# Second attention: the PSUM results of the side products are read one step later

## The chip, the cores and the metric

The kernel runs on one core of one Trainium2 chip. It is judged by its device time in microseconds (us), and the smaller is the better. Three runs of the kernel before gave 7818.84, 7816.00 and 7815.46 us; the median is 7816.0 us. One further execution was recorded by the hardware profiler: its time is 7809.57 us, and its span from the first instruction to the last is 7807.8 us.

## The reference

The program is a chain of four parts over 16 sequences of 512 tokens with 128 features. The change lies in the third part, which shares its stretch of time with the fourth.

```python
x = x + _L0_attn_ref(xn, ...) + _L0_ffn_ref(xn, ...)      # parts 1 and 2: four layers of scan + attention, ternary FFN
xn = _layernorm(x, axis=-1)
x = x + _L1_attn_ref(xn, ...) + _L1_ffn_ref(xn, Wr, W1, W2)

# part 3, _L1_attn_ref: 16 heads of 64, windows of 128 tokens
q, kv = x @ Wq, x @ Wkv                       # keys are also the values
q, kv = rotary(q) * SCALE, rotary(kv)
lkv = layernorm(look_around(kv))              # this window and the one before it
lsim = einsum('bwid,bwjd->bwij', q, lkv)      # masked: later tokens, before the start
pkv = softmax(kv by segments of 16 @ Wproj)   # one summary key for each segment
gkv = layernorm(sum of kv in a segment * pkv)
gsim = einsum('bnd,brd->bnr', q, gkv)         # masked: segments not finished
attn = softmax(concat([gsim, lsim]))
out = einsum(attn, concat([gkv, lkv])) @ Wout + bout

# part 4, _L1_ffn_ref: each token goes to one of 8 experts (argmax of softmax(x @ Wr)), at most 1024 for each
h = maximum(xe @ W1, 0);  ye = h @ W2         # xe: the tokens of one expert
y[token] = ye * p_token
```

## The kernel before

Parts 1 and 2 fill the first 5620 us and are not touched. Parts 3 and 4 are one block of code with an order written out by hand: the engines' queues hold the instructions in the order in which the Python code issues them, and each engine takes its queue in order.

Part 3 is cut into 64 **units** of 128 tokens (`u`; four of them, `t` = 0 to 3, make one sequence of 512), and a unit into four **groups** of four heads. The main loop runs over the groups `i`. In one turn it issues, with a call of `work(1)` after each piece:

- `scores(i)`: four matmuls `s` into PSUM tiles of pool `a_s` (five banks). VectorE reads each of them with the mask and takes the maximum (L1360, tiles `pr` and `am`), ScalarE makes the exponentials (L1361) and a copy `pg` of the summary columns (L1365). In a unit with `t` = 0 the rows are shorter.
- `weights_by_key(i - 1, two)`, twice: TensorE transposes (`gp` L1376 once, `pp` L1383), VectorE copies `gt` (L1378), ScalarE copies `pt` (L1385). `gp` and `pp` come from the same five banks as `s`; as seven tiles are taken in a turn, the first `pp` of a turn takes the bank of that turn's first `s`, and so waits until VectorE has read it.
- `values(i - 2, two)`, twice: the matmuls `o`, of which the first reads the summary values `gvb`; ScalarE copies `ot` (L1414) after every second group.

With a last `work(1)` this makes six steps in a turn and 24 in a unit.

Everything else is a **side product**, and is written as a generator in a list `streams`. `work(n)` goes through the list, resumes each generator that is due, and stops at the first one that answers with a positive number: that one has used the step. `yield 2` means "I have used this step; resume me two steps on", `yield -2` the same without using the step, `yield 0` "again at once". The generators, in the order of the list:

- `back(u)`: row sums to every lane by way of memory (`rd` L1424, L1426), then on GpSimd `ot` times their reciprocals (L1440), then the output projection: nine matmuls `po`, and VectorE's sum `ro` (L1447).
- `front(u)`: from the load of `xu` to the keys. Two products `kv` (read by VectorE, L1192 `by_cos`, and ScalarE, L1193 `raw`), four `q` (VectorE, L1210), GpSimd's rotary arithmetic (L1196 `raw`, L1199 and L1200 `kv`, L1218 `qt`), VectorE's `hm` (L1221) and `hd` (L1223), ScalarE's `hq` (L1229), GpSimd's `by_w` (L1227), VectorE's `hv` (L1232) and `pl` (L1244), the transposes `plt` (L1250, which reads `pl`; VectorE then makes `n` L1253, `smx` L1255 and `se` L1257) and `nt` (L1271, which read `n`; ScalarE L1272), `pwp` (L1283; VectorE `sw` L1285), the summary product `gp` into an `m` tile (VectorE L1298 to L1301), its norm on GpSimd (L1307 to L1314, tile `gv`), its transpose `gkt` (L1320; ScalarE L1327), and the DMAs `gv` (L1318) and `gvb` (four, L1333).
- `other_weights`, then `routing()`: it scatters the tokens to their experts (L1089, L1091) and then runs the 16 expert halves, each with one product `xep` (ScalarE L1122), four `hp` (ScalarE L1128) and one `yp` (VectorE L1135).
- `results()`, last: when the experts are done it gathers each token's expert row with a GpSimd DMA (`gy` L1147), loads `res` (L1154), adds them on VectorE (L1156) and stores `out` (L1157).

All side products share a pool of two banks, `a_m` (tiles `m_...`), in turn: a product can't begin until the product two before it has been read.

In the queues of the kernel before, the instructions that read a side product stand directly behind its matmuls, in the same resumption:

Of the kernel before, what the change touches and what calls it, by code (L numbers as in the profile page):

```python
# [69 lines left out]
def tile_kernel(  # L70
# [55 lines left out]
    with (  # L126
# [648 lines left out]
        tick = [0]  # L775
# [169 lines left out]
    with (  # L945
# [57 lines left out]
        def mm(out, lhsT, rhs, first=True, last=True):  # L1003
            nc.tensor.matmul(out, lhsT=lhsT, rhs=rhs, start=first, stop=last)  # L1004

        experts_done = [False]
        stored = [0]

        def routing():
# [8 lines left out]
            def big(i):  # L1018
                return space[:, i]
# [32 lines left out]
            total = misc("total")  # L1052
            mm(total, ones, hot2)
            tot = big(3)
            nc.vector.tensor_copy(tot, total.rearrange("p (t e) -> p t e", e=E))
            yield 1
            cum = pr.rearrange("p t e -> p (t e)").rearrange("p (e t) -> p e t", e=E)
# [7 lines left out]
            before = misc("before")  # L1065
            mm(before, const("tri"), hot2)
            rank = big(2)
            nc.vector.tensor_tensor(rank, cum.rearrange("p e t -> p t e"), tot, ALU.subtract)
            nc.vector.tensor_tensor(rank, rank, before.rearrange("p (t e) -> p t e", e=E), ALU.add)
            yield 1  # L1070
            nc.vector.tensor_tensor(rank, rank, hot, ALU.mult)
# [33 lines left out]
        def expert_half(e, hf):  # L1105
            nm = f"{e}_{hf}"
            if hf == 0:
                w1_sb = wk.tile([P, F1], F32, name=f"w1_{e}", tag="racc", bufs=1)
                nc.sync.dma_start(w1_sb, w1[e])
                w2_sb = wk.tile([P, 4, D], F32, name=f"w2_{e}", tag="x4", bufs=1)  # L1110
                nc.sync.dma_start(w2_sb, w2[e].rearrange("(c p) d -> p c d", p=P))
                expert_half.w = (w1_sb, w2_sb)
            w1_sb, w2_sb = expert_half.w
            at = e * CAP + hf * S
            xe = wk.tile([P, TB, D], F32, name=f"xe_{nm}", tag="x3", bufs=1)
            nc.sync.dma_start(xe, xe_d[at : at + S, :].rearrange("(t p) d -> p t d", p=P))
            yield -3
            ps = misc(f"xep_{nm}")
            for t in range(TB):
                nc.tensor.transpose(ps[:, t * P : (t + 1) * P], xe[:, t, :], ident)  # L1120
            xeT = wk.tile([P, S], F32, name=f"xeT_{nm}", tag="xt", bufs=1)
            nc.scalar.copy(xeT, ps)  # L1122
            yield 2
            he = wk.tile([P, 4, S], F32, name=f"he_{nm}", tag="he", bufs=1)
            for f in range(4):
                hp = misc(f"hp_{nm}_{f}")
                mm(hp, w1_sb[:, f * P : (f + 1) * P], xeT)
                nc.scalar.activation(he[:, f, :], hp, AF.Relu)  # L1128
                yield 1 + f // 3
            yp = misc(f"yp_{nm}")  # L1130
            for t in range(TB):
                for f in range(4):
                    mm(yp[:, t * P : (t + 1) * P], he[:, f, t * P : (t + 1) * P], w2_sb[:, f, :], f == 0, f == 3)
            ye = wk.tile([P, TB, D], F32, name=f"ye_{nm}", tag="d3", bufs=1)
            nc.vector.tensor_copy(ye, yp.rearrange("p (t d) -> p t d", d=D))  # L1135
            yield 2
            nc.sync.dma_start(ye_d[at : at + S, :].rearrange("(t p) d -> p t d", p=P), ye)
# [29 lines left out]
        def front(u):  # L1167
# [20 lines left out]
            for c in range(2):  # L1188
                ps = misc(f"kv_{u}_{c}")
                mm(ps, x, wkv_sb[:, c * S : (c + 1) * S])  # L1190
                psh = ps.rearrange("p (h d) -> p h d", d=DH1)
                nc.vector.tensor_tensor(halves(by_cos[:, 8 * c : 8 * c + 8]), halves(psh), table("cosk"), ALU.mult)  # L1192
                nc.scalar.copy(raw[:, 8 * c : 8 * c + 8], psh)  # L1193
                yield 1
            sink = const("sink")[:, t * 32 : (t + 1) * 32].unsqueeze(1).unsqueeze(1).broadcast_to(pair)
# [6 lines left out]
            for c in range(2):  # L1202
                parts = []
                for a, name in enumerate(("cosq", "sinq")):
                    ps = misc(f"q_{u}_{c}_{a}")
                    for i in range(4):
                        at = (4 * c + i) * P
                        mm(ps[:, i * P : (i + 1) * P], wq_sb[:, a, at : at + P], x)
                    q = wk.tile([P, 4, P], F32, name=f"q_{u}_{c}_{a}", tag=f"q{a}", bufs=2)
# [7 lines left out]
                    yield 1  # L1217
                nc.gpsimd.tensor_tensor(U.qt[:, 4 * c : 4 * c + 4, :], parts[0], parts[1], ALU.add)  # L1218
# [30 lines left out]
            ps = misc(f"plt_{u}")  # L1249
            nc.tensor.transpose(ps[0:H1, 0:P], pl, ident)  # L1250
            plv = ps[0:H1, 0:P].rearrange("p (s i) -> p s i", i=SEG)
            n = wk.tile(heads, F32, name=f"n_{u}", tag="hq", bufs=1)
# [6 lines left out]
            U.normed = True  # L1259
            yield 2  # L1260
            ss = wk.tile([H1, n_seg], F32, name=f"ss_{u}", tag="ss")
# [4 lines left out]
            for c in range(2):  # L1266
                ps = misc(f"nt_{u}_{c}")
                n2 = n.rearrange("p h d -> p (h d)")
                for i in range(4):
                    at = (4 * c + i) * P  # L1270
                    nc.tensor.transpose(ps[:, i * P : (i + 1) * P], n2[:, at : at + P], ident)  # L1271
                nc.scalar.activation(  # L1272
                    lkts[b % 2][:, 4 * c : 4 * c + 4, t * KW : t * KW + P],
                    ps.rearrange("p (i t) -> p i t", t=P),
                    AF.Identity,
                    scale=g_col,
                    bias=b_col,
                )
                yield 1
# [3 lines left out]
            nc.tensor.transpose(ps[:, 0:H1], se.rearrange("p s i -> p (s i)"), ident[0:H1, 0:H1])  # L1283
            sw = wk.tile([P, 4, 4, 32], F32, name=f"sw_{u}", tag="sw", bufs=1)
            nc.vector.tensor_tensor(  # L1285
# [4 lines left out]
            )  # L1290
            yield 2

            gp = misc(f"gp_{u}")
            for j in range(4):
                for g in range(4):
                    mm(gp[32 * g : 32 * g + 32, 0:DH1], sw[:, g, j, :], kv[:, 4 * g + j, :], j == 0, j == 3)
            gm = wk.tile([P, 1], F32, name=f"gm_{u}", tag="gm")
            nc.vector.tensor_reduce(gm, gp[:, 0:DH1], AX.X, ALU.add)  # L1298
# [4 lines left out]
            nc.scalar.activation(gq, gd, AF.Square, scale=DH1**-0.5)  # L1303
            yield 1
            gr = wk.tile([P, 1], F32, name=f"gr_{u}", tag="gr")
# [13 lines left out]
            ps = misc(f"gkt_{u}")  # L1319
            nc.tensor.transpose(ps[:, 0:P], gv.rearrange("p a d -> p (a d)"), ident)  # L1320
            for a in range(2):
                r = slice(64 * a, 64 * a + 64)
# [4 lines left out]
                nc.scalar.copy(to, keys.unsqueeze(2).broadcast_to([64, NHP, n, n_seg]))  # L1327
            yield 1
            yield -2
# [87 lines left out]
        def back(u):  # L1417
# [5 lines left out]
            ps = misc(f"rd_{u}")  # L1423
            nc.tensor.transpose(ps[0:H1, 0:P], U.sum, ident)  # L1424
            rd = wk.tile([H1, P], F32, name=f"rd_{u}", tag="rd", bufs=2)
            nc.vector.tensor_copy(rd, ps[0:H1, 0:P])  # L1426
            yield 2
            nc.sync.dma_start(rd_d[u % 2], rd)
# [14 lines left out]
            for i in range(NHP):  # L1443
                mm(po[:, 0:D], U.ot[:, i, :], wout_sb[:, i, :], i == 0, False)
            mm(po[:, 0:D], x1, ident, False, True)
            res = wk.tile([P, D], F32, name=f"ro_{u}", tag="ro", bufs=2)
            nc.vector.tensor_tensor(res, po[:, 0:D], bout_row, ALU.add)  # L1447
            yield 2
            nc.sync.dma_start(r_d[u * P : (u + 1) * P, :], res)
# [161 lines left out]
```

## Time and profile before

| What | Value |
|---|---|
| Median of three runs | 7816.0 us |
| Profiled execution: its time, its span | 7809.57 us, 7807.8 us |
| Parts 3 and 4: from about 5620 us to the end | some 2188 us |
| TensorE, VectorE, ScalarE, GpSimd busy, 7200 to 7400 us | 181.25, 133.06, 128.13, 142.45 us of 200 |
| The same, 6400 to 6600 us (experts running) | 189.36, 112.64, 123.06, 109.97 us of 200 |
| Granted TensorE clock, 6400 to 6600, 6800 to 7000, 7200 to 7400 us | 0.99, 0.86, 0.95 |

A line of the list of waits names who waited, for whom, the sum in us, how often and the longest. A line of the timeline gives the start, the length, the engine, the line, the operation and its tiles; the bracket is the engine's idle time before it and what ended it. A line of a table of stretches gives busy time and the number of instructions for each engine, and then the granted clock, where 1.00 is full speed.

### The profile page before, as it was taken

How to read it: one execution, taken by the hardware profiler on the slowest of the kernel's cores; microseconds unless marked ns; L12 is line 12 of the kernel's file. 1: busy time of each engine (PE TensorE's matmuls, PEld its weight loads, DVE VectorE, ACT ScalarE, POOL GpSimd, SP SyncE). 2: the span in 40 equal slices, each digit the busy share in tenths (PEclk: the TensorE clock that was granted, in tenths of full speed). 3: DMA queues.
4: the chain of work that ended last, by engine and by line, in shares of the span. 5: the costliest groups of instructions: out<-in, count | busy, mean ns of one | idle time of the engine just before them, and what ended most of it. 6: DMA issues, size and time to landing. Idle time of an engine off the chain costs nothing. (4 is left out here: it accounts for less than half of the span.)

```text
span 7807.8 us, 107882 instructions
## 1 busy us (share of the span) xinstructions
PE 7008.5 (90%) x38168; PEld 3232.4 (41%) x38168; DVE 4784.4 (61%) x9622; ACT 4616.8 (59%) x9357; POOL 3012.7 (39%) x3763
## 2 busy tenths in 40 slices
PE   6898999999999999999999999999678999888988
PEld 2233333333333333333333333333356666656666
DVE  4565666566666666566666666666366555666665
ACT  3565655666555666666666566656355666556666
POOL 3333332232223233222221222222268655667775
PEclk7899999999999999999999999999789999989999
DMA  2222222212222221122212222222211111111111
GB/s 70 78 83 65 75 70 66 84 64 69 68 71 69 70 66 64 65 64 71 69 61 65 66 74 80 77 77 91 78 33 50 49 42 49 40 46 32 34 35 36
DMA packets 394204, 491.18 MB, mean 63 GB/s; under 512 B 82240, under 2 KB 277952, under 8 KB 392512
## 3 DMA queue, kind: packets, MB, share of 16 engines
q1 hardware_dynamic: 389568, 475.89, 19.5%
q0 software_dynamic: 4096, 8.40, 0.4%
q8 instruction: 302, 4.95, 0.3%
q14 instruction: 238, 1.95, 0.1%
HBM read 348.35 MB, written 132.64 MB: 62 GB/s over the span
## 5 line engine op out<-in xcount | busy, mean ns | idle before, releaser
L921 DVE TENSOR_REDUCE nm<-n 128x1 f32<-128x512 f32 x4096 | 2588.3, 683 | 1459.5 <-PE n L177 1458.0
L923 ACT ACTIVATE pt<-t 128x512 f32<-128x512 f32 x4096 | 2215.3, 595 | 1871.7 <-PE t L177 1847.2
L177 PE MATMUL n<-kt,qt 72*128 72x512 bf16 x4096 | 1319.0, 388 | 200.5 <-DVE nm L921 158.8
L177 PE MATMUL t<-qt,kt 75*128 75x512 bf16 x4096 | 1351.7, 389 | 105.8 <-ACT pt L923 56.5
L177 PE MATMUL o<-pt,vt 128*32 128x512 f32 x8192 | 1131.8, 676 | 0.0
L177 PEld LDWEIGHTS <-qt 72*128 72x128 bf16 x4096 | 354.1, 98 | 1025.5 <-issue 881.3
L177 PEld LDWEIGHTS <-kt 75*128 75x128 bf16 x4096 | 399.2, 99 | 849.2 <-issue 518.3
L1361 ACT ACTIVATE pr<-pr,am 128x288 f32<-128x288 f32 (+1 forms) x1024 | 507.9, 498 | 211.5 <-DVE am L1360 210.6
L873 POOL CAST nmp<-nm 128x16 bf16<-128x16 f32 x256 | 49.9, 195 | 1451.7 <-DVE nm L921 1451.7
L177 PEld LDWEIGHTS o<-pt,vt 128*32 128x32 f32 x8192 | 231.9, 118 | 661.4 <-issue 527.1
L467 POOL TENSOR_TENSOR qk<-qk,parts 128x512 f32<-128x512 f32 x128 | 147.8, 1155 | 770.1 <-ACT parts L280 745.3
L1360 DVE CUSTOM_DVE_ANT_0 pr<-s,cst 128x288 f32<-128x288 f32 (+1 forms) x1024 | 373.0, 420 | 48.4 <-PE s L1004 47.6
L1383 PE MATMUL pp<-ident,pr 128*128 128x128 f32 x1792 | 311.9, 294 | 93.2 <-DVE am L1360 92.2
L1004 PE MATMUL o<-pt,lk 128*64 128x128 f32 x3584 | 328.5, 301 | 0.0
L1385 ACT COPY pt<-pp 128x512 f32<-128x512 f32 (+1 forms) x512 | 264.8, 526 | 97.0 <-PE pp L1383 95.4
L1210 DVE TENSOR_TENSOR q<-m_q,cst 128x512 f32<-128x512 f32 x256 | 177.1, 692 | 220.7 <-PE m_q L1004 220.7
L1004 PE MATMUL s<-lkt,qt 64*128 64x288 f32 (+1 forms) x2048 | 303.3, 414 | 0.4 <-ACT lkt L1327 0.4
L177 PE MATMUL m_in<-x,w 128*128 128x512 f32 x512 | 277.4, 627 | 17.1 <-POOL x L330 8.9
L1383 PEld LDWEIGHTS pp<-ident,pr 128*128 128x128 f32 x1792 | 215.0, 148 | 161.5 <-DVE am L1360 128.1
L1004 PE MATMUL m_q<-xu,wq_sb 128*128 128x128 f32 x2048 | 279.6, 280 | 1.3 <-ACT raw L1193 0.3
L177 PE MATMUL m_f<-n,w 128*128 128x512 f32 x512 | 272.5, 615 | 2.9 <-POOL n L330 2.6
L1004 PEld LDWEIGHTS m_q<-xu,wq_sb 128*128 128x128 f32 x2048 | 250.7, 193 | 19.3 <-ACT raw L1193 15.2
(336 smaller groups left out, 11103.9 us busy)
## 6 DMA issues: line engine op xcount, KB each, us to landing
qt<-q_d SPq DMA_DIRECT2D x768, 96.0 KB
kt<-k_d SPq DMA_DIRECT2D x256, 288.0 KB
rb_n<-rstd_d SPq DMA_DIRECT2D x64, 512.0 KB
rb<-rd SPq DMA_DIRECT2D x128, 256.0 KB
q_d<-parts SPq DMA_DIRECT2D x64, 384.0 KB
k_d<-parts SPq DMA_DIRECT2D x64, 384.0 KB
o_d<-og SPq DMA_DIRECT2D x512, 36.0 KB
oa<-o_d SPq DMA_DIRECT2D x64, 256.0 KB
```

The lines of the kernel that those rows point to most:

```text
L177: nc.tensor.matmul(out, lhsT=lhsT, rhs=rhs, start=first, stop=last)
L467: nc.gpsimd.tensor_tensor(x, x, parts[:, 0], ALU.subtract)
L873: nc.gpsimd.tensor_copy(parts[:, 0], nm)
L921: nc.vector.tensor_reduce(dst, n, AX.X, ALU.max, negate=True)
L923: nc.scalar.activation(dst, n, AF.Exp)
L1004: nc.tensor.matmul(out, lhsT=lhsT, rhs=rhs, start=first, stop=last)
L1210: nc.vector.tensor_tensor(q, ps.rearrange("p (i t) -> p i t", t=P), const(name)[:, t * P : (t + 1) * P].unsqueeze(1).broadcast_to([P, 4, P ...
L1360: nc.vector.tensor_tensor_reduce(pr[:, j, 0:n], s[:, 0:n], mask(t), -1.0, BIG, ALU.add, ALU.min, nmax)
L1361: nc.scalar.activation(pr[:, j, 0:n], pr[:, j, 0:n], AF.Exp, bias=nmax, scale=-1.0, accum_out=U.sum[:, 4 * g + j : 4 * g + j + 1])
L1383: nc.tensor.transpose(pp[:, a, c, :], G.pr[:, 2 * two + a, at : at + P], ident)
L1385: nc.scalar.copy(pt[:, :, 0:n, :], pp[:, :, 0:n, :])
```

## The change

Each generator of part 3 and 4 with a matmul into an `m` tile now stops between the matmul and the instructions that read it, with `yield TAKE`. This uses the step, as the positive number did. `work` keeps the generators that have stopped so in a list `held`, and resumes them first of all at its next call. Between the two calls the main loop issues its next piece, so that the reading instructions stand behind that piece's in the queues. The number after the reading instructions becomes the old one less one, with a minus where it isn't zero, so that most next steps are due when they were; the steps after `xep`, `yp`, `rd`, `po` and the summary product come one step later.

```diff
+        TAKE = 100
...
                 mm(ps, x, wkv_sb[:, c * S : (c + 1) * S])
+                yield TAKE
                 psh = ps.rearrange("p (h d) -> p h d", d=DH1)
                 nc.vector.tensor_tensor(halves(by_cos[:, 8 * c : 8 * c + 8]), halves(psh), table("cosk"), ALU.mult)
                 nc.scalar.copy(raw[:, 8 * c : 8 * c + 8], psh)
-                yield 1
+                yield 0
...
                         mm(ps[:, i * P : (i + 1) * P], wq_sb[:, a, at : at + P], x)
+                    yield TAKE
...
-                    yield 1
+                    yield 0
...
             nc.tensor.transpose(ps[0:H1, 0:P], pl, ident)
+            yield TAKE
...
             U.normed = True
-            yield 2
+            yield -1
...
                 mm(hp, w1_sb[:, f * P : (f + 1) * P], xeT)
+                yield TAKE
                 nc.scalar.activation(he[:, f, :], hp, AF.Relu)
-                yield 1 + f // 3
+                yield -(f // 3)
...
+            yield TAKE
             ye = wk.tile([P, TB, D], F32, name=f"ye_{nm}", tag="d3", bufs=1)
             nc.vector.tensor_copy(ye, yp.rearrange("p (t d) -> p t d", d=D))
-            yield 2
+            yield -2
...
             mm(po[:, 0:D], x1, ident, False, True)
+            yield TAKE
             res = wk.tile([P, D], F32, name=f"ro_{u}", tag="ro", bufs=2)
             nc.vector.tensor_tensor(res, po[:, 0:D], bout_row, ALU.add)
-            yield 2
+            yield -2
...
+        held = []
+
         def work(n):
+            for st in held:
+                st[1] = tick[0] + abs(next(st[0]))
+            held.clear()
             for st in list(streams):
                 if st[1] <= tick[0]:
                     wait = next(st[0], None)
                     if wait is None:
                         streams.remove(st)
+                    elif wait == TAKE:
+                        held.append(st)
+                        st[1] = tick[0] + 1
+                        n -= 1
+                        if n <= 0:
+                            break
                     elif wait:
                         st[1] = tick[0] + abs(wait)
                         n -= wait > 0
```

The same pair of edits is made at `total` and `before` (routing), `xep`, `nt`, `pwp`, the summary product, `gkt` and `rd`.

More of the change, by code (lines that the diff above doesn't have):

```diff
@@ L1193, in front @@
                 nc.scalar.copy(raw[:, 8 * c : 8 * c + 8], psh)
-                yield 1
+                yield 0
             sink = const("sink")[:, t * 32 : (t + 1) * 32].unsqueeze(1).unsqueeze(1).broadcast_to(pair)
@@ L1208, in front @@
                         mm(ps[:, i * P : (i + 1) * P], wq_sb[:, a, at : at + P], x)
+                    yield TAKE
                     q = wk.tile([P, 4, P], F32, name=f"q_{u}_{c}_{a}", tag=f"q{a}", bufs=2)
@@ L1216, in front @@
                     parts.append(q)
-                    yield 1
+                    yield 0
                 nc.gpsimd.tensor_tensor(U.qt[:, 4 * c : 4 * c + 4, :], parts[0], parts[1], ALU.add)
@@ L1250, in front @@
             nc.tensor.transpose(ps[0:H1, 0:P], pl, ident)
+            yield TAKE
             plv = ps[0:H1, 0:P].rearrange("p (s i) -> p s i", i=SEG)
@@ L1271, in front @@
                     nc.tensor.transpose(ps[:, i * P : (i + 1) * P], n2[:, at : at + P], ident)
+                yield TAKE
                 nc.scalar.activation(
@@ L1278, in front @@
                 )
-                yield 1
+                yield 0
             lk = U.lk
@@ L1283, in front @@
             nc.tensor.transpose(ps[:, 0:H1], se.rearrange("p s i -> p (s i)"), ident[0:H1, 0:H1])
+            yield TAKE
             sw = wk.tile([P, 4, 4, 32], F32, name=f"sw_{u}", tag="sw", bufs=1)
@@ L1290, in front @@
             )
-            yield 2
+            yield -1
             gp = misc(f"gp_{u}")
@@ L1296, in front @@
                     mm(gp[32 * g : 32 * g + 32, 0:DH1], sw[:, g, j, :], kv[:, 4 * g + j, :], j == 0, j == 3)
+            yield TAKE
             gm = wk.tile([P, 1], F32, name=f"gm_{u}", tag="gm")
@@ L1303, in front @@
             nc.scalar.activation(gq, gd, AF.Square, scale=DH1**-0.5)
-            yield 1
+            yield -1
             gr = wk.tile([P, 1], F32, name=f"gr_{u}", tag="gr")
@@ L1320, in front @@
             nc.tensor.transpose(ps[:, 0:P], gv.rearrange("p a d -> p (a d)"), ident)
+            yield TAKE
             for a in range(2):
@@ L1327, in front @@
                 nc.scalar.copy(to, keys.unsqueeze(2).broadcast_to([64, NHP, n, n_seg]))
-            yield 1
             yield -2
@@ L1424, in back @@
             nc.tensor.transpose(ps[0:H1, 0:P], U.sum, ident)
+            yield TAKE
             rd = wk.tile([H1, P], F32, name=f"rd_{u}", tag="rd", bufs=2)
             nc.vector.tensor_copy(rd, ps[0:H1, 0:P])
-            yield 2
+            yield -2
             nc.sync.dma_start(rd_d[u % 2], rd)
@@ L1445, in back @@
             mm(po[:, 0:D], x1, ident, False, True)
+            yield TAKE
             res = wk.tile([P, D], F32, name=f"ro_{u}", tag="ro", bufs=2)
             nc.vector.tensor_tensor(res, po[:, 0:D], bout_row, ALU.add)
-            yield 2
+            yield -2
             nc.sync.dma_start(r_d[u * P : (u + 1) * P, :], res)
```

## The prediction

> **What bounds the kernel now.** I began with the stretches of the page: TensorE has the highest share of busy time from 5800 us to the end.
>
> ```profile
> PE   6898999999999999999999999999678999888988
> POOL 3333332232223233222221222222268655667775
> PEclk7899999999999999999999999999789999989999
> ```
>
> The last 11 of the 40 columns (195 us each) are the stage of the change. TensorE is near 9 tenths, GpSimd no more than 8: what counts is what TensorE still waits for. So I asked for TensorE's waits in four stretches, cut where the side work changes: **A** 5838 to 6104 us (tokens are scattered), **B** 6138 to 6684 (experts), **C** 6684 to 7014 (results catch up), **D** 7044 to 7703 (steady).
>
> ```profile
> PE pp L1383 <- DVE am L1360: 20.7, 8, 2.9
> ...
> PE m_po L1004 <- POOL ot L1440: 15.7, 15, 1.9
> PE m_plt L1250 <- ACT he L1128: 8.6, 12, 0.7
> PE m_hp L1004 <- ACT he L1128: 3.9, 15, 0.3
> ...
> PE o L1004 <- DMA gvb<-gv: 32.5, 7, 5.2
> PE pp L1383 <- DVE am L1360: 14.0, 9, 2.6
> ...
> PE pp L1383 <- DVE am L1360: 35.4, 22, 2.1
> PE m_po L1004 <- POOL ot L1440: 21.4, 21, 1.9
> PE m_nt L1271 <- DVE se L1257: 12.5, 11, 1.4
> ```
>
> One line is from A, three from B, two from C, three from D. Per unit TensorE idles about 2 us in B and 3.2 in D ((35.4 + 21.4 + 12.5) / 22). No wait is for a side product's bank; the largest is for VectorE's late reading of `s`. The timeline shows why it is late, and the pace:
>
> ```profile
> 6465.10 0.29 DVE L1447 TENSOR_TENSOR ro<-m_po,rows_sb 128x128 f32<-128x128 f32 x1 [1.28 <-PE m_po L1004]
> 6501.89 0.29 DVE L1447 TENSOR_TENSOR ro<-m_po,rows_sb 128x128 f32<-128x128 f32 x1 [1.28 <-PE m_po L1004]
> ...
> 7284.48 0.29 DVE L1447 TENSOR_TENSOR ro<-m_po,rows_sb 128x128 f32<-128x128 f32 x1 [1.28 <-PE m_po L1004]
> 7284.68 1.21 DVE L1232 TENSOR_REDUCE hv<-hq 128x16 f32<-128x1024 f32 x1
> 7286.68 1.22 DVE L1244 TENSOR_REDUCE pl<-by_w 128x16 f32<-128x1024 f32 x1 [0.78 <-POOL by_w L1227]
> 7287.81 0.45 DVE L1360 CUSTOM_DVE_ANT_0 pr<-s,cst 128x288 f32<-128x288 f32 x1
> ...
> 7288.32 0.66 PE L1383 MATMUL pp<-ident,pr 128*128 128x128 f32 x4 [1.65 <-DVE am L1360]
> ...
> 7315.30 0.29 DVE L1447 TENSOR_TENSOR ro<-m_po,rows_sb 128x128 f32<-128x128 f32 x1 [1.28 <-PE m_po L1004]
> ```
>
> `ro` comes once in a unit: a unit takes 36.8 us in B and 30.8 in D (units with `t` = 0 about 2 less). In D `ro` waits for `po`, `hv` and `pl` stand behind it, `pl` waits for GpSimd's `by_w`, and the four `am` for all of them: TensorE loses 1.65 us.
>
> **The change, part by part.** No instruction is added or removed; I compared the built order of both kernels queue by queue. A steady unit has four turns on TensorE, after: [s gp pp o pp kv o kv q] [s q gp pp gkt o q pp q o] [s gp pp o pp po o plt] [s gp pp nt o nt pp pwp o rd gp]. Paces (start to start) from the D timeline: four `s` 1.17, `gp` 0.16, `pp` 0.5, `o` 0.9, `kv` 1.06, `q` 0.93, `po` 2.1, `nt` 0.55. Subtracting D's waits of a unit without a half-clock window (1.64 + 1.04 + 0.70) from its 30.5 leaves 27.1 us of work, before and after.
>
> *Third turn, scores.* VectorE's queue was [.. q q, am x4, gt hm hd ro hv pl, am x4]; it becomes [.. q q hm hd, am x4, gt hv pl ro, am x4]. The stall behind `pl` goes: `ro` no longer holds back `hv` and `pl`. But `hm` and `hd` now stand between the last `q` and the `am`. From that `q` matmul's end VectorE needs 0.1 + 0.68 (`q`) + 1.25 (`hm`) + 1.35 to 1.6 (`hd`; mean of D 1605 ns) + 0.5 (first `am`) = 3.9 to 4.1; TensorE needs `o` 0.9 + `s` 1.17 + `gp` 0.16 = 2.2 and then stands at `pp`: a stall of 1.6 to 1.9, for 1.65. Behind those `am` wait ScalarE's exponentials (also behind `hq`, 1.06), which have a turn of slack.
>
> *GpSimd.* Its queue becomes raw kv kv qt qt ot by_w (the second `qt` ahead of `ot`), and starts about 3.6 us earlier against the second turn's scores, as both `kv` now stand before the scores. `ot` is then ready when `po` comes: 0.7 saved. `by_w` ends 13.8 to 14.1 us after the second turn's start, `pl` 1.25 later; `plt`, now ahead of the fourth scores, is reached at 14.9: 0.3 lost.
>
> *Fourth turn.* `n` (1.1) now waits behind four `am`: 0.35 + 1.52 + 1.1 = 3.0 after `s` begins; TensorE reaches `nt` after 1.17 + 0.16 + 0.5 = 1.8. Stall 1.2, for 1.04. `rd` waits 0.2 for ScalarE's second reading of `nt`.
> D: 1.75 + 0.3 + 1.2 + 0.2 = 3.45, for 3.4: **about 0**, +3 us with rounding up over 22 units.
>
> *Clock.* Here a rule of the Trainium skill and the trace differ:
>
> ```profile
> 7282.16 2.05 PE L1004 MATMUL m_po<-wout_sb,ot 128*128 128x128 f32 x16 [0.70 <-POOL ot L1440]
> ...
> 7285.18:7288.30 3.12, 1.50 (x11) 0.82 (x9) 2.34 (x5) 0.52 (x2) 2.62 (x7) 1.00 0.15 42
> ...
> 7289.73:7293.35 3.62, 3.62 (x22) 2.89 (x20) 2.58 (x8) 2.51 (x9) 0.00 (x0) 0.53 0.08 20
> ```
>
> After the 1.65 us stall TensorE ran 3.6 us at clock 0.53, and the work took some 1.4 us longer than at full clock (o, plt, pp, o, rd: 7139.09 to 7142.42 less its wait of 1.04 is 2.3). "TensorE: Matmul & The Clock Gate" (Part 1, What's actually happening) says that the clock halves after at least one idle window of about 3.4 us. By that rule no stall here would cost clock; by the row one of 1.65 us can, when it falls inside a window. I take the row. Such a window also gives VectorE time: the unit with it lasts 30.8, without `nt`'s stall, and the unit without it 30.5. After, stalls are as long: 0, and 1.4 more for each unit in which a window falls where none did.
>
> *Experts (B).* One half costs TensorE 8.1 us (in the timeline from 6574.4 us on: `xep` 0.6, four `hp` at 0.96, `yp` 3.7). Before: one half in every unit, and its products stand where the stalls were, so a unit with it is only 6.2 longer (36.8 less 30.6). After: halves take 30 steps instead of 24 (two later steps, and steps lost to `front`), so 16 halves spread over 18.75 units instead of 15, and fall on different turns from unit to unit. Over a cycle of five units (four halves) I count stalls, by the sums above: third turn 0, 1.3, 1.75, 2.6 (VectorE's `ye` ahead of `hm`, `hd`), 0; fourth turn 1.2, 0.75, 0.75, 1.2, 1.2; `hp` waiting for `he`, which is queued behind `hq` and four exponentials, 1.7 once; 1.2 more of small bank waits: 13.7, or 2.7 a unit, and two half-clock windows, 0.55 a unit. 27.1 + 0.8 x 8.1 + 2.7 + 0.55 = 36.9. So 3.75 units run at 36.9 instead of 30.6: **+24 us**. "PSUM — Partial Sum Buffer" (Summary: rules for kernel authors) says to empty PSUM promptly, which speaks against this change; the trace has no bank wait now, and my sum has 1.7 + 1.2 us of it in five units (11 us in 18.75 units). If it bit at every product it would be far more; the alternating two banks leave a whole step.
>
> *Catching up (C).* Before, `gvb` stands on SP behind an `out` that waits for `res` (SP is idle for it up to 9 us), and `o` waits 32.5 us in all. After, two `gvb` go ahead of that `out`, two behind one that only waits for a `res` right after the last `q`: hidden, as `o` needs them 5 us later. But VectorE now has `pl res ro res` before the fourth `am`; the second `res` needs a gather that GpSimd issues after `by_w` (1.1 us, and 2.6 to land): about 3 us late, so TensorE waits 2.8 at `pp` and 1.7 at `nt`. Unit: 27.1 + third turn 2.0 + po, plt 1.2 + 2.8 + 1.7 + 0.3 = 35.1, with half-clock windows about 36.5 (t = 0: 34.5), for a mean of 36.6 now (330 us, 9 units). 10.5 units instead of 9.25 (backlog 32 for 28, three gained a unit): 10.5 x 36.0 = 378 against 338.6 + 1.25 x 30.2 = 376: +2. Without the late gather it would be about -44, with one us more of it +12; as the lower end is the farther, I take -4.
>
> *Scatter (A).* GpSimd's queue is nearly without gaps (33.1 us a unit) and keeps the same instructions: 0. Start and end of the stage: a step of one VectorE instruction later, below 1.
>
> **Sum**: D +3, B +24, C -4, A 0: +23. On the profiled execution's own time (7809.6; 1.8 of it lies outside the span) that gives 7832.6; the median of the runs stood 6.4 above it, so **7839 us**. Where stalls go, what is late next is VectorE again, one turn earlier.
>
> **Rivals.**
> *The stalls do go (faster, 7766).* If the gathers of C land before VectorE comes to the second `res`, C loses 2.8 + 1.4 us in 10.5 units, -40 against my -4; if `hp` in other turns fills stalls as now, B is +9 rather than +24; D -15 rather than +3 (0.7 a unit). 7839 - 73. For it: 230 us of waits are there to take. Against: `hm` + `hd` are 2.6 us, more than the 2.2 of TensorE work that covers them. It decides where `hd` ends within 2.2 us of the last `q`.
> *VectorE and GpSimd collide (much slower, 7901).* `hd` now runs beside `qt` and `ot`; it takes up to 2.29 us elsewhere in the trace. One us more in some 47 units of B, C, D, and a half-clock window in a third more of the units (1.4 x 11): +62, so 7901.
> *It does nothing (7816).* The stall moves and B's spreading is free, as units of D keep idle time for it.
>
> **How the numbers follow.** Forecast 0.40 (its own range 7825 to 7860), faster rival 0.25, collision 0.17, nothing 0.18. 0.2% is 15.6 us, about what can be told from no change. Slower: 0.40 + 0.17, less 0.03 at the edge: 0.54; same 0.20; faster 0.26. Range 7765 to 7900.
>
> **What would show it.** Right: `pp <- am` at about 1.7 us a unit with `hd` before the `am`; `o <- gvb` gone; `po <- ot` gone; experts ending some 140 us later; `nt <- se` or `n` at 1.2. Wrong: D units below 30 us, or waits of `kv`, `q`, `hp` for their banks of over 1 us a unit.

## The result and the profile after

The changed kernel takes **7901.42 us** (median of four runs, 7896.19 to 7916.08) against 7815.73 us for the kernel before (7813.78 to 7818.84): a ratio of 1.0113, with a 95% interval from 1.0098 to 1.0128. It is 86 us slower. The forecast was 7839 us and its range ended at 7900. The profiled execution took 7903.82 us, its span 7902.0 us.

The two profiles are best compared by `ro`, which comes once in a unit, counted from the first `kv` product (5627.64 us before, 5639.24 after; parts 1 and 2, which nothing touched, differ by those 11.6 us, and this is left out). How far the kernel after lies behind, and what the prediction had for it:

| Stretch (units) | Predicted | Measured |
|---|---|---|
| start, to unit 3 | under 1 | +13.6 |
| scatter, 3 to 12 | 0 | +20.8 |
| experts, 12 to 31 | +20 with the next row (B +24, C -4) | -6.3 |
| catching up, 31 to 42 | in the row above | +33.7 |
| steady, 42 to the end | +3 | +20.8 |
| sum | +23 | +82.6 |

The two middle rows can be set against the prediction only as a sum, which is +27.4. They do not hold the same work: before, units 28 to 36 catch up, so that four of these fall into the first row and six steady units (37 to 42) into the second; after, every unit of the first row belongs to the experts and every one of the second (32 to 42) catches up.

On the page of the kernel after, the same three rows, in slices of 198 us; the stage of the change is the last 11 or 12 columns. TensorE starts the stage at 5, 7, 7 and 8 tenths where it had 6, 7 and 8, and GpSimd shows 7 where it had 8, in the scatter.

```profile
PE   6898999999999999999999999999577899888888
POOL 3333233232223232222222222222377555566675
PEclk8999999999999999999999999999789999989999
```

TensorE's waits in the stage after, from 5600 us on (sum, times, longest, in us):

```profile
PE pp L1395 <- DVE am L1372: 122.9, 62, 8.8
PE m_nt L1280 <- DVE n L1262: 84.6, 54, 1.9
...
PE m_q L1004 <- ACT raw L1200: 23.9, 34, 1.5
PE m_po L1004 <- POOL ot L1453: 20.1, 21, 4.1
PE m_gkt L1332 <- DVE q L1218: 14.1, 60, 0.3
```

The wait for `gvb` has gone from the head of the list and that for `ot` has fallen from 66.9 to 20.1 us; the prediction had both gone. In their place stand `nt` waiting for `n`, and two waits that the prediction's sums did not have: `q` waiting for ScalarE's `raw`, and `gkt` for the bank of a `q`. The steady part alone, units 44 to 62 (7328.8 to 7876.3 us):

```profile
PE m_nt L1280 <- DVE n L1262: 26.7, 17, 1.6
PE pp L1395 <- DVE am L1372: 24.6, 16, 1.9
PE m_q L1004 <- ACT raw L1200: 7.9, 12, 1.1
PE m_plt L1258 <- DVE pl L1252: 6.1, 12, 0.7
PE m_gkt L1332 <- DVE q L1218: 3.8, 16, 0.3
PE m_po L1004 <- POOL ot L1453: 2.0, 5, 0.6
```

With two small rows that is 73.3 us in 18 units, 4.07 a unit. The same 18 units before: `pp` 26.0, `po` 16.7, `nt` 7.3, others 1.5, together 51.5, or 2.86 a unit. The difference, 22 us, is about what these units lost (547.5 us for 528.2); TensorE was busy in them for 474.2 us, and for 476.3 before. The timeline shows the two largest of them where the prediction had them:

```profile
7569.48 0.69 DVE L1218 TENSOR_TENSOR q<-m_q,cst 128x512 f32<-128x512 f32 x1 [0.64 <-PE m_q L1004]
7570.08 1.21 DVE L1229 TENSOR_REDUCE hm<-kv 128x16 f32<-128x1024 f32 x1
7571.33 1.27 DVE L1231 SCALAR_TENSOR_TENSOR hd<-hm,kv 128x1024 f32<-128x1024 f32 x1
...
7573.03 0.66 PE L1395 MATMUL pp<-ident,pr 128*128 128x128 f32 x4 [1.57 <-DVE am L1372]
...
7575.31 3.19 PE L1004 MATMUL m_po<-wout_sb,ot 128*128 128x128 f32 x16
...
7583.26 0.66 PE L1280 MATMUL m_nt<-ident,n 128*128 128x128 f32 x4 [1.61 <-DVE n L1262]
```

In the third turn `hm` and `hd` stand between the last `q` and the first `am`, and `pp` waits 1.57 us. In the fourth, `n` (1.22 us) stands behind four `am`, and `nt` waits 1.61.

### The profile page after: what moved, and what is told of

Its sections match the earlier page's. It is cut to its first block, busy times and chain, and to the rows that moved or that the text cites. A ratio compares the mean times of both kernels' runs of the same rounds, so it can differ in the third digit from the quotient of the medians.

```text
span 7902.0 us, 108007 instructions
## 1 busy us (share of the span) xinstructions
PE 7023.6 (89%) x38168; PEld 3239.6 (41%) x38168; DVE 4746.9 (60%) x9622; ACT 4608.4 (58%) x9357; POOL 3018.7 (38%) x3763
## 5 line engine op out<-in xcount | busy, mean ns | idle before, releaser
L1395 PE MATMUL pp<-ident,pr 128*128 128x128 f32 x1792 | 312.8, 294 | 125.0 <-DVE am L1372 122.9
L1004 PE MATMUL m_q<-xu,wq_sb 128*128 128x128 f32 x2048 | 289.2, 285 | 25.0 <-ACT raw L1200 23.9
```

The costliest lines, as they stand in the source:

```text
L1395: nc.tensor.transpose(pp[:, a, c, :], G.pr[:, 2 * two + a, at : at + P], ident)
```

## The experiments

The built orders say something that the diff does not: the change has two parts. **Late taking** is one. The other is a **phase**: the one step that the summary product `gp` takes longer sets, in the first units, where the fronts stand against the main loop, and from then on they stay there. The steady order on TensorE, turn by turn:

```
old phase   s*4 nt gp pp pwp o pp gp o kv | s*4 kv gp pp q o q pp q o gkt q
(before)    s*4 gp pp o pp po o           | s*4 gp pp o plt pp o rd nt
new phase   s*4 gp pp o pp kv o kv q      | s*4 q gp pp gkt o q pp q o
(after)     s*4 gp pp o pp po o plt       | s*4 gp pp nt o nt pp pwp o rd gp
```

(A `gp` behind the scores is the weights' transpose; the one behind `pp` or `rd` is the summary product.) Whether a product is taken late and in which phase it stands can be chosen apart. So there were two theories: P, that the phase is the loss, and T, that late taking is.

**Phase alone** (`o_shift`): the kernel before, one number changed.

```diff
             nc.scalar.activation(gq, gd, AF.Square, scale=DH1**-0.5)
-            yield 1
+            yield 2
```

> The kernel before with one number changed: the summary product's side stream waits two steps instead of one after its square, and nothing is taken later. In the built order this alone puts the fronts (kv, q and what follows) as far ahead of the main loop as in the kernel after. Theory P (the loss comes from this phase of the fronts against the main loop, an accident of the one added step at the summary product): 7880 to 7905 us, units of the steady part at 31 to 32 us with nt waiting for n. Rival T (the loss comes from products being taken late): 7805 to 7825, as before. If both have a part: near 7850.

Measured: 7847.58 us, ratio 1.0049 (1.0033 to 1.0064), as expected if both have a part.

**Late taking in the old phase** (`u_shift`): the kernel after, one number changed.

```diff
             nc.scalar.activation(gq, gd, AF.Square, scale=DH1**-0.5)
-            yield -1
+            yield 0
```

> The kernel after with one number changed: behind the summary product's square the stream goes on in the same step in which it would have gone on before. Every product is still taken one step late; the fronts keep the phase of the kernel before. Theory P: 7800 to 7830 us. Rival T: 7880 to 7905.

Measured: 8071.9 us, ratio 1.0332 (1.0311 to 1.0352). Neither theory holds alone. Late taking costs 259 us in the old phase (3.32% of 7816) and, with the new phase, 86: the phase alone costs some 38 us, but saves most of what late taking would cost without it. The waits of this kernel:

```profile
PE m_pwp L1293 <- ACT lkt L1282: 123.2, 60, 2.7
PE pp L1395 <- DVE am L1372: 95.5, 48, 6.3
PE m_q L1004 <- ACT raw L1200: 87.1, 61, 1.5
```

Its timeline in one steady unit shows what `lkt`, the copy of `nt`, is late for:

```profile
7681.17 0.63 PE L1280 MATMUL m_nt<-ident,n 128*128 128x128 f32 x4
7681.73 1.24 PE L1004 MATMUL s<-lkt,qt 64*128 64x288 f32 x8
...
7684.59 0.52 ACT L1373 ACTIVATE pr<-pr,am 128x288 f32<-128x288 f32 x1
...
7685.44 0.77 ACT L1282 ACTIVATE lkt<-m_nt,rows_sb 128x512 f32<-128x512 f32 x1
...
7686.35 0.20 PE L1293 MATMUL m_pwp<-ident,se 16*128 16x16 f32 x1 [2.47 <-ACT lkt L1282]
```

The first `nt` is the last piece of its turn. A step later means behind the next turn's scores, so its copy stands behind four exponentials on ScalarE, and `pwp`, the second next product, waits 2.47 us for the bank. `kv` is the last piece of another turn, and `q` waits for its `raw` in the same way.

**The same with `nt` and `kv` taken at once** (`u_sntkv`).

```diff
             nc.tensor.transpose(ps[:, i * P : (i + 1) * P], n2[:, at : at + P], ident)
-                yield TAKE
...
-                yield 0
+                yield 1
```

and the same for `kv`.

> The kernel with all late takes in the phase of before (8072 us), with two kinds of product taken at once again: nt and kv. Theory K (there each late copy of nt and of kv stands on ScalarE behind four exponentials, and the second next product, pwp or q, stands at the bank: 123.2 us at pwp, 87.1 at q): both waits go and 7850 to 7880 is left. Rival (the time is lost to the late n, sum and results, and the two waits only show it): 7950 or more.

Measured: 7818.12 us, ratio 1.0001 (0.9990 to 1.0012), less than either expectation. All that late taking costs in the old phase are these two kinds: 254 us between the two kernels. That is 44 more than their two waits (123.2 and 87.1), which come with a slower TensorE (granted clock 0.92, 0.89 and 0.93 in units 12 to 33, 33 to 44 and 44 to 62, for 0.96, 0.95 and 0.95 before). All other products, `plt`, `pwp`, the summary, `gkt`, `q`, the experts', `rd` and `po`, can together be taken late in the old phase at no cost, and with no gain. The last `q` is among them, though it too ends a turn: the next but one product, which needs its bank, is a `plt` two turns on, while `pwp` and `q` come in the very next turn. The list of this kernel has `lkt` in it only with 1.3 us, and at its head the waits of before:

```profile
PE pp L1393 <- DVE am L1370: 87.9, 48, 6.5
PE m_po L1004 <- POOL ot L1451: 54.6, 39, 3.6
PE o L1004 <- DMA gvb<-gv: 43.4, 9, 5.9
PE m_nt L1279 <- DVE se L1265: 33.6, 32, 1.4
```

In the new phase other products come last in their turns: a `q`, `plt` and the summary product (see the orders above). The next runs undo these in the kernel after, one by one.

**`plt` at once** (`u_plt`): its `yield TAKE` removed, and `yield -1` behind `se` made `yield 2`.

> The kernel after with the segment weights' transpose (plt) taken at once: n, smx and the difference for se stand before the fourth turn's four am instead of behind them. Phase and all other late products stay. If n behind the am is what costs (1.6 us a unit in 54 waits of nt, 85 us): nt stops waiting, but pp waits about 1 more, so 7860 to 7880. If it is only exchanged for a wait of the same am: 7895 to 7910.

Measured: 7892.03 us, ratio 1.0094 (1.0074 to 1.0115). The wait of `nt` for `n` is gone (1.6 us left of 84.6), but `pp` waits 165.1 for `am` where it waited 122.9, and `pwp` 31.2 for `lkt`, where it waited 1.2. Mostly an exchange: the interval overlaps with that of the kernel after.

**The summary product at once, phase kept** (`n_gp`).

```diff
                     mm(gp[32 * g : 32 * g + 32, 0:DH1], sw[:, g, j, :], kv[:, 4 * g + j, :], j == 0, j == 3)
-            yield TAKE
...
             nc.scalar.activation(gq, gd, AF.Square, scale=DH1**-0.5)
-            yield -1
+            yield 2
```

> The kernel after with the summary product taken at once and its next step kept two steps away, so that the order on TensorE in the steady part stays that of the kernel after. Only gm, gd and gq move back, ahead of the next turn's scores' work. Theory G (in the scatter GpSimd is the bound, and what it loses is its wait for gr: 7.5 us before, 22.1 with the phase alone, 29.9 after, 37.8 with the summary product alone late): gr's wait falls by some 10 us, and q's wait for raw (0.5 us a unit, raw stands behind gq and gd on ScalarE) goes in the steady part too: -10 to -15 in the scatter, -15 in the 40 units behind, 7870 to 7880. Rival: raw stands behind the exponentials in any case: 7885 to 7895.

Measured: 7869.22 us, ratio 1.0053 (1.0037 to 1.0070), the largest single part. The scatter falls from 319.9 to 313.8 us, less than expected, and the wait for `raw` is gone from the steady part. Units 44 to 62 take 19 us less, of which the waits are only 7.6. Here are these units after, then in this kernel, then in `u_exp`, a kernel below whose steady order is that of the kernel after (stretch, its length, TensorE busy with its instructions, four more engines' busy times, granted clock, DMA share, GB/s):

```profile
7328.79:7876.26 547.47, 474.23 (x4113) 353.11 (x4113) 336.23 (x1051) 340.12 (x1027) 361.92 (x333) 0.97 0.13 34
```

```profile
7309.24:7837.73 528.49, 462.73 (x4113) 347.29 (x4113) 334.70 (x1052) 341.42 (x1027) 362.29 (x333) 0.98 0.14 35
```

```profile
7344.86:7882.98 538.12, 465.38 (x4113) 345.93 (x4113) 335.87 (x1052) 339.66 (x1027) 361.73 (x333) 0.98 0.13 34
```

The same 4113 matmuls took 11.5 us longer after than in `n_gp`, at a lower granted clock. The waits do not explain this: `u_exp` has 72.8 us of them here, for 73.3 after, with the summary late as well, and took 465.4 us. So some 9 of the 11.5 us can't be put down to the late summary; they came with that one profiled execution, and why stays open. The chain that delays `raw` in a steady unit after:

```profile
7557.84 0.22 DVE L1310 TENSOR_REDUCE gm<-m_gp 128x1 f32<-128x64 f32 x1
...
7559.25 0.25 ACT L1315 ACTIVATE gq<-gd 128x64 f32<-128x64 f32 x1
7559.53 0.22 DVE L1318 TENSOR_REDUCE gr<-gq 128x1 f32<-128x64 f32 x1 [0.51 <-ACT gq L1315]
7559.84 0.22 POOL L1319 TENSOR_SCALAR gr<-gr 128x1 f32<-128x1 f32 x1 [3.88 <-DVE gr L1318]
...
7560.75 0.35 ACT L1324 ACTIVATE gd<-gd,gr 128x64 f32<-128x64 f32 x1 [1.00 <-POOL gr L1320]
...
7561.26 1.07 ACT L1200 COPY raw<-m_kv 128x512 f32<-128x512 f32 x2
7561.90 1.16 PE L1004 MATMUL m_q<-xu,wq_sb 128*128 128x128 f32 x8 [1.15 <-ACT raw L1200]
```

`gm` waits behind four `am`, `gq` behind four exponentials, GpSimd 3.88 us for `gr`, ScalarE a further 1.00 us for GpSimd, with `raw` behind it, and TensorE 1.15 us for `raw`.

**The summary product and `plt` at once** (`n_gpplt`): both edits.

> The kernel after with the summary product and plt taken at once, in the phase of the kernel after; against the kernel with kv and q at once as well (7830 us) it tells what late kv and q cost. If plt is what was won there (n behind four am): 7830 to 7840. If late kv and q cost it (gkt waits 0.26 us for q, raw moves): 7855 to 7865.

Measured: 7845.05 us, ratio 1.0034 (1.0025 to 1.0042), between the two expectations.

**These two, `kv` and `q` at once** (`n_early`): both edits, and for `kv` and `q` `yield TAKE` removed and `yield 0` made `yield 1`.

> The kernel after with four kinds of product taken at once again (kv, q, plt and the summary product), in the phase of the kernel after; experts, nt, pwp, rd, gkt and the results stay late. The steady order becomes that of the phase alone (29.0 us a unit against 30.4), -25 us there, and the scatter loses the wait for gr that the late taking adds, -8. If late taking of the experts costs nothing: 7850 to 7865. If it costs what the stretch from unit 12 to 44 lost (27 us) it stays in: 7865 to 7880.

Measured: 7830.02 us, ratio 1.0011 (1.0002 to 1.0020): 20 us below the lowest value expected. So, in this order of undoing, late `kv` and `q` cost some 18 us, `plt` some 15, the summary some 47: the ratio falls by 0.0023, 0.0019 and 0.0060 along this row of kernels. For `plt` the two intervals overlap, for the others they do not. The steady units take 28.84 us, for 29.35 before and 30.42 after.

**The summary product alone late** (`o_gp`): the kernel before with that one `yield TAKE`, and `yield -1` for `yield 1` behind the square. It has the new phase.

> The kernel before with the summary product alone taken one step late (its reduction, difference and square behind the next turn's scores and weights), all other products taken at once. It has the new phase, and GpSimd's wait for gr. Theory P with gr: 7890 to 7910 us, with GpSimd waiting some 3 us a unit for gr during the scatter (20 us in all) and the rest from the phase. Rival T: only the wait for gr, 7835.

Measured: 7876.21 us, ratio 1.0074 (1.0055 to 1.0093), a little under the expectation of P, and 0.0025 above the phase alone (some 20 us; the two intervals overlap). In the scatter it is the slowest of all kernels, at 333.7 us. What GpSimd waits for there:

```profile
POOL gr L1309 <- DVE gr L1308: 37.8, 9, 5.1
POOL xe_d L1092 <- DMA xe_d<-xts,slot: 24.7, 16, 1.6
```

**The experts' products at once** (`u_exp`): the three `yield TAKE` of `xep`, `hp` and `yp` removed from the kernel after, and their old numbers restored.

> The kernel after with the experts' products alone taken at once again (a half takes fewer steps). Theory S (the experts' late takes spread the halves over more units and so put off the catching up, which is where TensorE's waits rise by 24 us): the last half ends some 100 us earlier, and 7875 to 7885. Rival (the waits of the catching up come from the order of its units, not from when it begins): 7895 to 7905.

Measured: 7916.32 us, ratio 1.0121 (1.0107 to 1.0136). The last half did end 80 us earlier (1129 us into the stage for 1209), but the kernel is no faster: the ratio is 0.0008 higher than that of the kernel after, within the intervals. So the theory that the spread of the halves puts off the catching up and so costs time falls. There are fewer units with a half, but each takes longer (units 13 to 27: 39.3 us in the mean; after, units 13 to 31: 36.0).

**The experts' products alone late, new phase** (`p_exp`): the kernel before with those three `yield TAKE`, and `yield 2` behind the square.

> The kernel before in the phase of the kernel after, with the experts' products alone taken late. Taking these at once made the kernel after 15 us slower. If their late taking is the gain of the kernel with four kinds at once over the phase alone (14 us of this stage): 7825 to 7835. If the gain came from nt, pwp, rd, gkt or the results: 7845 to 7855.

Measured: 7825.11 us, ratio 1.0010 (0.9998 to 1.0022), as the first expectation has it. In the new phase, late taking of the experts' products wins some 30 us (0.49% less 0.10%), and it alone brings the phase to where the kernel with four kinds at once stands. Undone from the kernel after (`u_exp`) the same late taking was worth nothing that can be told; what a part is worth depends on what else is late.

**GpSimd's wait for `gr`** (`a_gr`, and in the kernel before as a control `b_gr`).

```diff
             nc.vector.tensor_reduce(gr, gq, AX.X, ALU.add)
-            nc.gpsimd.tensor_scalar(gr, gr, EPS1, None, ALU.add)
-            nc.gpsimd.tensor_tensor(gr, gr, neg_half[:, 0:1], ALU.pow)
+            nc.scalar.activation(gr, gr, AF.Ln, bias=eps1[:, 0:1])
+            nc.scalar.activation(gr, gr, AF.Exp, scale=-0.5)
```

> The kernel after with the summary's reciprocal root (gr: add, then power, two small GpSimd instructions behind VectorE's reduction) done by two small ScalarE activations, a logarithm and an exponential; GpSimd no longer has an instruction that waits for the reduction, only the later gd for the scaled gd. If the wait for gr is what the scatter loses: GpSimd's wait there falls from 29.9 us to under 10 in nine units, the scatter takes 300 to 310 us instead of 320, and the whole 7880 to 7890; q's wait for raw changes by less than 0.3 us a unit. If GpSimd loses the time by being fed late in any case (the wait moves to gd, raw or xe_d): scatter 315 to 325, whole 7895 to 7910.

> The control: the same edit in the kernel before, whose GpSimd waits only 7.5 us for gr in the scatter. 295 to 303 us in the scatter (299 before), whole within 10 us of before, if what the edit wins is the wait; if two GpSimd instructions less are worth something of their own, it shows here too.

Measured: 7869.99 us, ratio 1.0075 (1.0059 to 1.0091), and for the control 7811.03 us, 0.9993 (0.9984 to 1.0002). In the scatter of `a_gr`:

```profile
POOL gd L1325 <- ACT gd L1324: 21.7, 9, 3.7
...
POOL raw L1203 <- ACT raw L1200: 8.3, 8, 2.4
```

The wait moved to `gd`, and the scatter took 317.5 us for 319.9: there the second expectation holds, and GpSimd is fed late whichever instruction meets the lateness first. Even so the whole is some 30 us faster, more than either expectation. The profile puts 9.4 us of this in the start and 14 in the steady part, where the chain to `raw` is shorter: the wait of `q` for `raw` falls from 7.9 to 4.3 us. TensorE's busy time falls from 474.2 to 463.2 us, but most of that `u_exp` has too, without the edit. In the control, where `q` does not wait behind that chain, the edit is worth nothing that can be told.

**New phase from unit 22 on** (`o_late`), and **experts late with the new phase from unit 10 on** (`best10`), both from the kernel before, to find a faster one:

```diff
-            yield 1
+            yield 4 if u == 22 else 2 if u > 22 else 1
```

(with 10 in the place of 22 for the second).

> The kernel before, with the phase of the fronts moved to that of the kernel after from unit 22 on alone (three steps more at that unit's summary product, one more at each later one); no product taken late. The phase alone lost 35 us up to unit 24 (16 of them in the scatter) and won 16 behind it: 7795 to 7805 us, steady units at 29.0 against 29.4. If the gain of the phase in the steady part was bought by the earlier loss (work put off): 7810 to 7820.

> The kernel before with the experts' products alone taken late, and the new phase from unit 10 on (three steps more at that unit's summary product, one more at each later one); the scatter before it keeps the order of before. By the parts: start and scatter as before, then -17 from unit 12 to the end: 7795 to 7810 us, faster than both. If the phase wins behind only what it loses ahead of it: 7815 to 7825.

Measured: 7825.85 us, ratio 1.0001 (0.9990 to 1.0012), and 7820.93 us, 1.0003 (0.9992 to 1.0013). Neither beats the kernel before. Their profiles also tell how far a single one can be trusted: the scatter took 307 and 309 us in these two, whose order is that of before for most or all of it, and 299 to 301 us in the kernel before, `u_sntkv` and `b_gr`. And the profiled execution of `o_shift` lies 13 us below the median of its runs, so that its sum below is +20 where the ratio says +38.

Where each kernel stands against the kernel before in its own profile, in us, counted as in the first table, with what GpSimd waits for `gr` in the scatter (in `a_gr` and `b_gr` for `gd`). As above, 12-31 and 31-42 hold different work where the experts are late, and only their sum compares:

| Kernel | start | scatter | (GpSimd waits) | 12-31 | 31-42 | 42-end | sum |
|---|---|---|---|---|---|---|---|
| before | 0 | 0 | 7.5 | 0 | 0 | 0 | 0 |
| `u_sntkv` | -1 | +2 | 8.9 | -6 | +6 | +6 | +7 |
| `b_gr` | -4 | +1 | 2.2 | +3 | -2 | +2 | -1 |
| `best10` | +4 | +10 | 7.4 | -22 | +24 | -6 | +10 |
| `o_late` | +4 | +8 | 16.8 | +8 | -7 | -3 | +10 |
| `n_early` | +6 | +17 | 22.1 | -31 | +23 | -9 | +6 |
| `p_exp` | +4 | +14 | 19.2 | -26 | +24 | -7 | +10 |
| `o_shift` | +4 | +17 | 22.1 | +13 | -7 | -7 | +20 |
| `n_gpplt` | +7 | +26 | 23.7 | -24 | +22 | -7 | +24 |
| `n_gp` | +12 | +15 | 20.9 | -6 | +27 | +1 | +48 |
| `a_gr` | +4 | +19 | 21.7 | -6 | +32 | +7 | +56 |
| `o_gp` | +9 | +35 | 37.8 | +24 | -3 | +5 | +68 |
| `u_plt` | +10 | +30 | 37.4 | -12 | +32 | +10 | +71 |
| after | +14 | +21 | 29.9 | -6 | +34 | +21 | +83 |
| `u_exp` | +16 | +23 | 31.0 | +43 | +5 | +11 | +99 |
| `u_shift` | +7 | +20 | 23.0 | +85 | +55 | +89 | +256 |

## Why the prediction was wrong

By the ratios, and in one order of undoing, the 86 us are made of: the phase, +38; late experts' products in that phase, -30; late `q` and `kv`, +18; late `plt`, +15; the late summary product, +47 (88 in all; the rest changes nothing that can be told). In another order the sizes differ, as `o_gp` and `u_exp` show.

**The step that failed is the late summary product, put at nothing.** In the prediction's own list of the new order it is the last piece of the fourth turn, so that what reads it stands behind the next turn's scores; the prediction followed `hm`, `hd`, `pl` and `n` through the queues, but had no term for this chain anywhere. Taken at once, it gives back 47 us by the ratios (1.0113 to 1.0053, intervals apart). In the profiles the four kernels that take it late in the new phase, its root on GpSimd (`o_gp`, `u_plt`, after, `u_exp`), lie 68 to 99 us behind the kernel before, the five in that phase that take it at once (`o_shift`, `p_exp`, `n_early`, `n_gpplt`, `n_gp`) 6 to 48. In the means of the two groups the start is at +12 for +7, the scatter at +27 for +18, the units from 42 on at +12 for -6.

**A, "nearly without gaps ... the same instructions: 0".** It was +20.8, and most of it comes with the phase, which alone has +17. The instructions are the same, but GpSimd comes to `gr` before VectorE and ScalarE have made it: that wait went from 7.5 to 29.9 us. Nor was the queue nearly without gaps: GpSimd's waits in the scatter were 53 us in all before, of 299, and 75 after. Among the kernels of the table the wait for `gr` and the length of the scatter go together in rough steps: about 303 us in the old order, with 2 to 17 us of this wait; 317 in the new phase, with 19 to 24; 326 with the summary late as well, with 30 to 38 (`u_shift`, with other waits besides, left out). That GpSimd is the bound there, so that the wait is the loss, is argued from this. Taking `gr` itself away only moved the wait, so a test that frees GpSimd of all lateness was not made.

**D, "3.45, for 3.4: about 0".** It was 4.07 for 2.86 (in units 44 to 62). The after side missed two terms: `q` waiting for `raw`, 0.44 a unit, behind the summary's chain, and `gkt` for a `q`'s bank, 0.21; and `nt` was sized at 1.2 and waited 1.48. Its `plt`, 0.34, was right, its `pp` 0.4 too long (1.37 for 1.75). The larger error was on the before side: the sum took a unit that shows all three stalls (1.64, 1.04 and 0.70) for every unit, while `nt` stood still in only 6 of 18 units and cost 0.41 in the mean. The lines of waits that the prediction itself showed gave 69.3 us in 22 units, 3.15, as the better base.

**Start, "below 1".** It was +13.6. In the new phase the second unit's `plt`, for which TensorE waits 6.6 us, stands ahead of the first scores, as does a `gkt` that waits 4.6; the first scores come at 44.8 us of the stage for 33.2, in the phase alone too. The phase alone has caught up all but 4 us by unit 3, in the kernel after 14 are left.

**B and C.** Their sum, +20, was near (+27.4), and so were their counts: the last half ends 169 us later, for "some 140", the halves lie in units 12 to 31 for 12 to 27 before, and the catching up takes some 10.5 units for 9, where the prediction had 10.5 for 9.25. A unit with the halves took 36.0 us for 36.9 forecast, a unit of the catching up (32 to 41) 36.4 for 36.0, and the second `res` did wait for its gather, 2.6 us in the mean. But the reason given for B does not hold: in the new phase the runs show the experts' late taking as a gain or as nothing, not as a loss of 24. In units 12 to 33 TensorE's granted clock was 0.98, for 0.94 with the experts at once; that a half's products then fall on different turns from unit to unit would fit, but was not tested.

**The rivals.** The faster one asked that `hd` end within 2.2 us of the last `q`; it ended 3.2 us behind it (7572.60 us), and `pp` waited; its parts also sum to 69 us and not 73. "VectorE and GpSimd collide" named the time, 7901, by luck, for its cause did not come: `hd` ran in 1.47 us in the mean, for 1.71 before, and `qt` in 1.27 during the scatter, for 1.77; neither took longer.

**The two rules of the Trainium skill.** "PSUM — Partial Sum Buffer" (Summary: rules for kernel authors) wants PSUM emptied promptly. The prediction read its lines as showing no bank wait, but two of them are such waits: `plt` and `hp` behind `he`, 8.6 and 3.9 us in B, since `he` is what empties the bank that they need. It set the bank waits that come of the change at 11 us, in B. Measured in the whole stage after: `q` for `raw` 23.9, `gkt` for `q` 14.1, `hp` and `po` for `he` 10.9, some 49 us, where the same list before has 13 for `he` and next to nothing for `raw` and `q`. In the old phase the same edit has 210 us of them. So the rule mattered for `nt` and `kv`, whose banks are needed again in the next turn; for the others taken together it made no difference (ratio 1.0001). "TensorE: Matmul & The Clock Gate" (Part 1, What's actually happening) has the clock halve after an idle window of about 3.4 us, and by that no stall here would cost clock; the row that the prediction chose instead was right: after, a stall of 1.57 us at `pp` is followed by a `po` of 3.19 us at a granted clock of 0.59, for 2.05 at full clock. But a stall has no fixed price in clock: in the kernel before, the 1.65 us that end at 7137.69 us are followed by 3.4 us at 1.00, and in units 44 to 62 `u_exp` ran its matmuls 9 us faster than the kernel after with as much waiting.

## What to carry to other kernels

An instruction that is moved "one step later" is moved past whatever the program issues in that step: where the product ends its turn, that is four maxima and four exponentials. It cost most where the bank or the value is needed again early in the next turn. So look first at the few products that end a turn, and follow each one's chain through every engine to the next use of its bank and of its value. Where an order comes out of a scheduler, separate the edit from the shift of phase that it brings (one number in one generator here), because the shift can matter as much as the edit: here it cost 38 us by itself and saved 173 of what late taking would have cost; and take the base of a sum from a mean over the stretch, not from the unit that shows every stall.

## What the runs showed that was not expected

The phase is a state that the first units set, and it stays. One step more at every unit's summary product from the first unit on gives the new phase; the same from unit 22 on leaves the old one in the built order (but for `gkt` and the last `q`, which change places; this was not run); three steps more once, and one at each later unit, move it over.

A shorter chain of tiny instructions was worth 0.38% of the kernel: `a_gr` replaced two GpSimd instructions of 0.22 and 0.57 us by two on ScalarE and won some 30 us by the ratios (1.0113 to 1.0075, intervals apart). In the kernel before, the same edit won nothing. Where the 30 us lie is not settled by the one profile of each kernel.
